# Expert blocks of an attention and mixture-of-experts kernel: the gathered inputs are transposed by VectorE instead of TensorE

## Chip, cores and metric

The kernel runs on one core of one Trainium2 chip. The metric is the device time of one execution in microseconds. Time before: 920.09 us, the median of six runs (919.37 to 922.16).

## What is computed

The reference is one layer in fp32 on `x` of shape (4, 1024, 256): cross attention with a residual, then a mixture of experts with a residual. Only the second half matters here. Of nine experts each token takes the two with the highest probabilities, with weights that add to one:

```python
xf = x.reshape(T, H)                      # layer-normalised, T = 4096, H = 256
cw = zeros((T, E)).at[arange(T)[:, None], idxf].add(wf)      # E = 9, two entries per token
gate = silu(einsum('th,ehi->tei', xf, Wg))                   # i = 704
hidden = gate * einsum('th,ehi->tei', xf, Wu)
out = einsum('tei,eih,te->th', hidden, Wd, cw)
```

## The kernel before

**Attention stage** (the first 387 us of the span). The tokens go by in 32 steps of 128. After each group of 512 tokens, `choices` finds the two experts of each token, `places` (L936) works out where each token stands in the list of its expert, and GpSimd writes token number and weight there by indirect DMA (L950). The normalised tokens go to a DRAM buffer, `y_d`.

**Expert stage** (from 387 us). The lists are cut into blocks, and each block is worked for one expert. A "pair" block (2 in `blocks[j][0]`) has 256 tokens, a "one" block 128; a "flex" block is a one block whose two halves of 64 tokens belong to two experts. There are 41 in the main order: blocks 0 to 5 are pairs ("early", whose lists are known before the last group's), then fifteen times a pair and a one (blocks 6 to 35), then the pairs 36 to 40. One more flex block, `NBLK`, runs only if the counts ask for it.

Each block j goes through these steps:
- `tokens(j)`: GpSimd gathers the token numbers and weights of the block into `ids`. `inputs(j)`: GpSimd gathers the tokens' rows out of `y_d` into `yin` (L1183), one indirect DMA for each 128 tokens, into one of three buffers. `weights(j)`: SyncE loads the expert's weights, `wgu` and `wd`, in six DMAs. All are issued by `fetch()`, which runs at the start of each block: inputs and weights two blocks ahead, tokens four ahead. GpSimd's queue is in order, and also has the scatters of the lists and of the results.
- `turn(j)` (L1202): TensorE transposes `yin`, which has tokens on partitions, by a product with the identity, in squares of 128 (L1211): four for a pair, two for a one. ScalarE copies them from PSUM (tile `px`) to `xT` (L1214), which has features on partitions and two buffers.
- `hidden_pair(j)` (L1218): for f = 0 to 5, four matmuls (two for f = 5) into `pg` (L1225), Silu on ScalarE (L1231), and the product on VectorE (L1232; L1235 for f = 5) into `hid`. `pg` rotates over five PSUM banks. After each f, `pump()` runs up to six steps of `rest`: the routing of the last 512 tokens and then `late_blocks` (L1054), both chains of small VectorE operations. `rest` is empty at the end of block 4.
- `hidden_one(j)` (L1249): three wide products, `psg`, `psu` and `psb`, with 128 tokens as the stationary operand; Silu, and three products on VectorE, of which the last is L1271. `hidden_turn(j)` (L1275) transposes the result on TensorE (L1282) and copies it to `hid`, one half on ScalarE and one on VectorE (L1285).
- `down(j)` (L1289): the second products into `po` (L1299); VectorE multiplies by the token's weight into `co` (L1302). `adding` (L1331): GpSimd adds `co` to the output rows by indirect DMA (L1334).

The order is written out by hand, and each engine follows its own part of it. A step j of the main loop (L1515) is: `fetch()`, hidden products of block j, `turn(j + 1)`, `split(j + 1)` (two small VectorE operations for a flex block, L1319), `down(j - 1)`, `adding` of block j - 1, and for a one block `hidden_turn(j)`. Block 0 is turned inside the last attention step (L1454) and block 1 just behind it (L1503).

Of the kernel before, what the change touches and what calls it, by code (L numbers as in the profile page):

```python
# [15 lines left out]
P = 128  # L16
# [5 lines left out]
def kernel(  # L22
# [18 lines left out]
    nc = tc.nc  # L41
# [82 lines left out]
    def mm_tile(name):  # L124
        return ps_mm.tile([P, TB], F32, tag="mm", name=name)
# [230 lines left out]
    with ExitStack() as kvs:  # L356
# [152 lines left out]
        def place_of(n, t):  # L509

            k, q = divmod(n, N2)
            return (2 * q + t) * 2 + k
# [133 lines left out]
        for n in range(NP):  # L646
# [6 lines left out]
            for c in range(C):  # L653
                for t in range(2):
# [6 lines left out]
                    h = place_of(n, t)  # L661
# [431 lines left out]
    blocks = [(2, i, "early") for i in range(EARLY)]  # L1093
# [12 lines left out]
    hids, wds, yins, ids = [], [], [], []  # L1106
    late = {}

    def of(tiles, j):

        return tiles[j % len(tiles)] if j < NBLK else late[id(tiles)]
# [45 lines left out]
    def weights_upper(j):  # L1157

        _, i, kind = blocks[j]
        if kind == "flex":  # L1160
            load(tabs[kind][0][0:1, 2 * i + 1 : 2 * i + 2], late["w2"], late["d2"])

    def load(number, w, d):
        e = nc.values_load(number, engines=[mybir.EngineType.SP], min_val=0, max_val=E - 1)
        wg_v = wg.rearrange("e (c p) f -> e p c f", p=P)[bass.ds(e, 1)].rearrange("o p c f -> (o p) c f")
        wu_v = wu.rearrange("e (c p) f -> e p c f", p=P)[bass.ds(e, 1)].rearrange("o p c f -> (o p) c f")


        nc.sync.dma_start(out=w[:, :, 0:FF], in_=wg_v)
        nc.sync.dma_start(out=w[:, :, FF : FF + FT], in_=wu_v[:, :, NF * P :])  # L1170
        nc.sync.dma_start(out=w[:, :, FF + FT : FF + FB], in_=wu_v[:, :, FA : NF * P])
        nc.sync.dma_start(out=w[:, :, FF + FB :], in_=wu_v[:, :, 0:FA])
        nc.sync.dma_start(
            out=d[:, 0:NF, :],
            in_=wd[bass.ds(e, 1), 0 : NF * P, :].rearrange("o (f p) d -> p (o f) d", p=P),
        )
        nc.sync.dma_start(
            out=d[64:128, NF, :], in_=wd[bass.ds(e, 1), NF * P : FF, :].rearrange("o p d -> (o p) d")
        )
# [8 lines left out]
    def tokens(j):  # L1188

        nh, i, kind = blocks[j]  # L1190
        got = gather(
            ids[j].rearrange("p h t -> p (h t)"), lists[nh], tabs[kind][1][:, i : i + 1]
        )
        if j in (0, EARLY):
            after(got, sent, "all places of the lists")
# [3 lines left out]
            bound = TOK if j >= EARLY else G_EARLY * TB  # L1199
            gather(of(yins, j)[:, h, :], y_d[:bound, :], ids[j][:, h, 0:1], bound)  # L1200

    def turn(j):  # L1202

        nh = blocks[j][0]
        xT = xTs[j] = late["xT"] if j >= NBLK else pools["spool"].tile(
            [P, C, TS], F32, tag="xT", name=f"xT{j}"
        )
        px = ps_sc.tile([P, TB], F32, tag="sc0", name=f"px{j}").rearrange("p (c t) -> p c t", c=C)
        for c in range(C):
            for h in range(nh):  # L1210
                nc.tensor.transpose(  # L1211
                    px[:, c, h * P : (h + 1) * P], of(yins, j)[:, h, c * P : (c + 1) * P], ident
                )
        nc.scalar.copy(xT[:, :, : nh * P], px[:, :, : nh * P])  # L1214

    UP = [FF + FB + f * P for f in range(FA // P)] + [FF + FT + f * P for f in range(NF - FA // P)]

    def hidden_pair(j, also={}):  # L1218

        (w,), xT, hid = wgus.pop(j), xTs.pop(j), hids[j % 2]  # L1220
        for f in range(NF + 1):
            pg = mm_tile(f"pg{j}_{f}").rearrange("p (g t) -> p g t", g=2)
            for g, at in enumerate((f * P, UP[f]) if f < NF else (f * P,)):
                for c in range(C):
                    nc.tensor.matmul(  # L1225
                        pg[:, g, :], w[:, c, at : at + P], xT[:, c, :],
                        start=(c == 0), stop=(c == C - 1),
                    )
            sl = pools["spool"].tile([P, TS], F32, tag="sl", name=f"sl{j}_{f}")
            if f < NF:  # L1230
                nc.scalar.activation(sl, pg[:, 0, :], AF.Silu)  # L1231
                nc.vector.tensor_tensor(hid[:, f, :], pg[:, 1, :], sl, ALU.mult)  # L1232
            else:
                nc.scalar.activation(sl[64:128, :], pg[0:64, 0, :], AF.Silu)
                nc.vector.tensor_tensor(  # L1235
                    hid[64:128, NF, :], pg[64:128, 0, :], sl[64:128, :], ALU.mult
                )
            pump()
            for fn in also.get(f, ()):
                fn()  # L1240

# [2 lines left out]
    def lanes(of_experts):  # L1244

        n = P // len(of_experts)
        return [slice(h * n, (h + 1) * n) for h in range(len(of_experts))]

    def hidden_one(j):  # L1249


        ws, xT = wgus.pop(j), xTs.pop(j)
        hs = hss[j] = late["hs"] if j >= NBLK else pools["spool"].tile(
            [P, FF], F32, tag="hs", name=f"hs{j}", bufs=1
        )
        pgs = {}
        for k, (at, n) in (("g", (0, FA)), ("u", (FF + FB, FA)), ("b", (FA, 2 * FB))):
            pgs[k] = mm_tile(f"ps{k}{j}")
            for c in range(C):
                for w, rows in zip(ws, lanes(ws)):  # L1260
                    nc.tensor.matmul(
                        pgs[k][rows, :n], xT[:, c, rows], w[:, c, at : at + n],
                        start=(c == 0), stop=(c == C - 1),
                    )
        nc.scalar.activation(hs[:, :FA], pgs["g"], AF.Silu)
        nc.vector.tensor_tensor(hs[:, :FA], pgs["u"], hs[:, :FA], ALU.mult)
        nc.scalar.activation(hs[:, FA:], pgs["b"][:, :FB], AF.Silu)
        nc.vector.tensor_tensor(
            hs[:, FA : NF * P], pgs["b"][:, FB + FT : 2 * FB], hs[:, FA : NF * P], ALU.mult
        )  # L1270
        nc.vector.tensor_tensor(  # L1271
            hs[:, NF * P :], pgs["b"][:, FB : FB + FT], hs[:, NF * P :], ALU.mult
        )
# [53 lines left out]
    def rounds_of(j):  # L1327
        n = 2 if blocks[j][2] == "flex" else 1
        return [(j, rows) for rows in lanes(range(n))]
# [18 lines left out]
    def pump():  # L1348

        if held[0]:  # L1350
            held[0] -= 1
            return
        for _ in range(STEP if rest else 0):
            got = next(rest[0], None)
            if got is None:
                rest.pop(0)
                if not rest:
                    fetch()
                return
            if got is PRODUCT:  # L1360
                held[0] = HOLD
                return
# [3 lines left out]
    def fetch():  # L1366

        end = NBLK if late_ready() else EARLY
        for name, fn, lead in (
            ("weights", weights, LEAD), ("weights_upper", weights_upper, LEAD + 1),  # L1370
            ("inputs", inputs, LEAD), ("tokens", tokens, LEAD + 2),
        ):
            if name == "inputs":

                while ahead["tokens"] < min(now[0] + LEAD + 1, end):
                    tokens(ahead["tokens"])
                    ahead["tokens"] += 1
            while ahead[name] < min(now[0] + lead + 1, end):
                fn(ahead[name])
                ahead[name] += 1  # L1380
# [8 lines left out]
    def advance(what, n=None):  # L1389

        for _ in range(n) if n is not None else iter(int, 1):
            if next(what, None) is None:
                return True
        return False
# [18 lines left out]
    for i in range(N_SUB + 1):  # L1413
        g, s = divmod(i, NS)
        now_on = i < N_SUB
        q = g - 1
# [98 lines left out]
    for j in range(LAST):  # L1515
        now[0] = j
        if j == EARLY:
            assert not rest
            open_late()
        fetch()  # L1520
        if j == EARLY + 1:
            count = nc.values_load(
                tabs["flex_total"][0:1, 0:1], min_val=0, max_val=2 * FLEX
            )
        if j == RARE_AT - 1:
            tokens(NBLK)
            inputs(NBLK)
        if j == RARE_AT:
            weights(NBLK)
            weights_upper(NBLK)  # L1530
        if blocks[j][0] == 2:
            hidden_pair(j)
        else:
            hidden_one(j)
        if j:
            turn(j + 1)
            split(j + 1)
            down(j - 1)
            for r in rounds_of(j - 1):
                adding(*r)  # L1540
        if blocks[j][0] == 1:
            hidden_turn(j)
        if j == RARE_AT:
            split(NBLK)

            with tc.If(count > 2 * (FLEX - RARE)):  # L1546
                turn(NBLK)
                hidden_one(NBLK)
                hidden_turn(NBLK)
                down(NBLK)  # L1550
            for r in rounds_of(NBLK):
                adding(*r)
# [37 lines left out]
```

## Time and profile before

| | |
|---|---|
| median of six runs | 920.09 us (919.37 to 922.16) |
| the profiled execution's own time | 917.93 us |
| its span (first to last instruction) | 916.2 us |
| mean granted TensorE clock | 0.998 |
| ScalarE copies px to xT | x41, 372 to 618 ns each |
| gathers of yin, issue to landing | 2.7 / 5.0 / 7.2 us (least, median, most) |
| expert stage, 500 to 600 us: busy TensorE, VectorE, ScalarE, GpSimd | 100.0, 25.3, 19.9, 45.3 us |
| same stretch, DMA share and rate | 0.82, 236 GB/s |

PE is TensorE's matmuls, PEld its weight loads, DVE VectorE, ACT ScalarE, POOL GpSimd, SP SyncE. L1211 is line 1211 of the kernel before. A line of a timeline has the start in microseconds, the duration, the engine, the line, the operation, output <- inputs, how many instructions were merged into it, and in brackets the idle time in front of it with what ended that. Every fp32 matmul of the hidden and down products has two records. Tile names are given without the block's number. The slices of the page are 40 equal parts of the span, 22.9 us each.

### The profile page before, as it was taken

How to read it: one execution, taken by the hardware profiler on the slowest of the kernel's cores; microseconds unless marked ns; L12 is line 12 of the kernel's file. 1: busy time of each engine (PE TensorE's matmuls, PEld its weight loads, DVE VectorE, ACT ScalarE, POOL GpSimd, SP SyncE). 2: the span in 40 equal slices, each digit the busy share in tenths (PEclk: the TensorE clock that was granted, in tenths of full speed). 3: DMA queues.
4: the chain of work that ended last, by engine and by line, in shares of the span. 5: the costliest groups of instructions: out<-in, count | busy, mean ns of one | idle time of the engine just before them, and what ended most of it. 6: DMA issues, size and time to landing. Idle time of an engine off the chain costs nothing. (4 is left out here: it accounts for less than half of the span.)

```text
span 916.2 us, 13532 instructions
## 1 busy us (share of the span) xinstructions
PE 900.9 (98%) x4290; PEld 694.7 (76%) x4290; DVE 442.8 (48%) x1310; ACT 334.5 (37%) x1055; POOL 316.3 (35%) x328
## 2 busy tenths in 40 slices
PE   8999999999999999999999999999999999999996
PEld 6647777777777777788888777777778778888885
DVE  5775688878788987654622222222222222222221
ACT  4557556564656557441211212211222222221210
POOL 3000002141404343065554435435435435444422
PEclk9999999999999999999999999999999999999999
DMA  7011010521202600466779769779779777779822
GB/s 264 2 23 41 24 47 25 47 46 24 70 24 66 217 24 25 132 188 153 190 217 291 214 207 309 216 210 318 216 209 306 219 200 224 223 219 315 226 29 23
DMA packets 110374, 137.92 MB, mean 151 GB/s; under 512 B 24663, under 2 KB 80287, under 8 KB 110304
## 3 DMA queue, kind: packets, MB, share of 16 engines
q1 hardware_dynamic: 92746, 119.66, 42.8%
q0 software_dynamic: 17344, 17.26, 10.5%
q8 instruction: 35, 0.57, 0.3%
q14 instruction: 35, 0.29, 0.2%
q10 hardware_dynamic: 214, 0.13, 0.0%
HBM read 119.48 MB, written 18.33 MB: 150 GB/s over the span
## 5 line engine op out<-in xcount | busy, mean ns | idle before, releaser
L1225 PE MATMUL pg<-xT,wgu 128*128 128x256 f32 x1144 | 251.8, 380 | 0.4 <-PEq L1546 0.4
L1225 PEld LDWEIGHTS pg<-xT,wgu 128*128 128x128 f32 x1144 | 216.3, 190 | 28.9 <-issue 0.8
L1299 PE MATMUL po<-wd,hid 128*128 128x256 f32 (+1 forms) x804 | 180.5, 380 | 0.0
L1299 PEld LDWEIGHTS po<-wd,hid 128*128 128x128 f32 (+1 forms) x804 | 147.5, 187 | 21.0 <-issue 0.7
L277 ACT ACTIVATE ex<-psc,mx 128x77 f32<-128x77 f32 x512 | 123.6, 360 | 102.4 <-DVE mx L267 101.2
L1334 POOL DMA_INDIRECT out_dram<-co,ids x63 | 100.7, 1598 | 169.6 <-DVE co L1302 147.8
L950 POOL DMA_INDIRECT list_d<-r_entry,r_pli x64 | 68.8, 1075 | 247.6 <-issue 124.1
L336 PE MATMUL po<-u,aT 128*128 128x265 f32 x640 | 151.7, 391 | 0.4
L263 PE MATMUL psc<-g,zT 128*128 128x462 f32 (+1 forms) x384 | 139.2, 511 | 0.0
L336 PEld LDWEIGHTS po<-u,aT 128*128 128x128 f32 x640 | 118.9, 190 | 23.1 <-ACT aT L325 1.4
L1232 DVE TENSOR_TENSOR hid<-pg,sl 128x256 f32<-128x256 f32 x130 | 55.1, 424 | 160.2 <-ACT sl L1231 160.0
L1231 ACT ACTIVATE sl<-pg 128x256 f32<-128x256 f32 x130 | 49.7, 383 | 218.4 <-PE pg L1225 213.4
L263 PEld LDWEIGHTS psc<-g,zT 128*128 128x128 f32 x384 | 72.5, 190 | 58.1 <-issue 50.5
L1302 DVE TENSOR_SCALAR co<-po,ids 128x256 f32<-128x256 f32 x67 | 32.4, 484 | 136.5 <-PE po L1299 134.3
L1183 POOL DMA_INDIRECT yin<-y_d,ids x67 | 70.3, 1049 | 25.1 <-issue 14.7
L267 DVE TENSOR_REDUCE mx<-psc 128x6 f32<-128x462 f32 (+1 forms) x96 | 55.7, 581 | 19.1 <-PE psc L263 16.4
L297 DVE TENSOR_REDUCE sm<-ex 128x16 f32<-128x1232 f32 x32 | 45.9, 1435 | 36.4 <-ACT ex L277 36.4
L325 ACT COPY aT<-pa 128x512 f32<-128x512 f32 (+1 forms) x96 | 49.4, 553 | 26.3 <-PE pa L317 26.3
L317 PEld LDWEIGHTS pa<-ident,an 128*128 128x128 f32 x320 | 36.7, 141 | 8.1 <-PE po L336 1.4
L317 PE MATMUL pa<-ident,an 128*128 128x128 f32 x320 | 40.3, 273 | 1.0 <-DVE an L301 1.0
L301 DVE TENSOR_TENSOR an<-ex,rs 128x1024 f32<-128x1024 f32 x32 | 39.2, 1225 | 1.1
L1287 ACT COPY hid<-ph 128x384 f32<-128x384 f32 x15 | 7.2, 478 | 73.9 <-PE ph L1282 73.9
(311 smaller groups left out, 803.4 us busy)
## 6 DMA issues: line engine op xcount, KB each, us to landing
wgu<-in_L_ffn_Wg_dram SPq DMA_DIRECT2D x41, 704.0 KB
wd<-in_L_ffn_Wd_dram SPq DMA_DIRECT2D x41, 640.0 KB
wgu<-in_L_ffn_Wu_dram SPq DMA_DIRECT2D x41, 512.0 KB
wgu<-in_L_ffn_Wu_dram SPq DMA_DIRECT2D x41, 128.0 KB
x<-in_x_dram SPq DMA_DIRECT2D x8, 512.0 KB
out_dram<-x SPq DMA_DIRECT2D x8, 512.0 KB
y_d<-y SPq DMA_DIRECT2D x8, 512.0 KB
w<-in_L_ffn_Wg_dram SPq DMA_DIRECT2D x5, 704.0 KB
```

What stands on the lines that cost most here:

```text
L263: nc.tensor.matmul(psc[:, :w], zT[:, c, :], g_sb[i // NS // GPB][:, c, h * J : h * J + w], start=(c == 0), stop=(c == C - 1),)
L267: nc.vector.tensor_reduce(nmx[i][:, h : h + n], psc[:, : n * J].rearrange("p (h j) -> p h j", h=n), AX.X, ALU.max, negate=True,)
L277: nc.scalar.activation(exs[i][:, h + q, :], pscs[k][:, q * J : (q + 1) * J], AF.Exp, bias=nmx[i][:, h + q : h + q + 1],)
L317: nc.tensor.transpose(pa[:, q * P : (q + 1) * P], ans[i][:, (k + q) * P : (k + q + 1) * P], ident)
L336: nc.tensor.matmul(po[:, :DE], aT[:, n, :], u_sb[b][:, n, :], start=(n == 0), stop=(n == KC - 1))
L950: i = nc.gpsimd.indirect_dma_start(out=list_d[:, :], out_offset=bass.IndirectOffsetOnAxis(ap=place_i[:, s : s + 1], axis=0), in_=entries[k ...
L1183: return nc.gpsimd.indirect_dma_start(out=dst, out_offset=None, in_=src, in_offset=bass.IndirectOffsetOnAxis(ap=offsets, axis=0), **kw,)
L1225: nc.tensor.matmul(pg[:, g, :], w[:, c, at : at + P], xT[:, c, :], start=(c == 0), stop=(c == C - 1),)
L1231: nc.scalar.activation(sl, pg[:, 0, :], AF.Silu)
L1232: nc.vector.tensor_tensor(hid[:, f, :], pg[:, 1, :], sl, ALU.mult)
L1299: nc.tensor.matmul(po[rows, :D], hid[:, f, at], d[:, f, :], start=(f == 0), stop=(f == NF))
L1334: i = nc.gpsimd.indirect_dma_start(out=out_r, out_offset=bass.IndirectOffsetOnAxis(ap=rows_of(j, h, rows), axis=0), in_=cos[j][:, h, :], i ...
```

## The change

From block 2 on, `turn(j + 1)` in the main loop is replaced by a generator, `turning(j + 1)`. It issues 16 VectorE transposes, one for each square of 32 partitions by 32 partitions: each instruction reads 32 partitions (tokens a to a + 31) of `yin` and writes 32 partitions (features q to q + 31) of `xT`, for both column halves c and, in a pair, both token halves h. That is 128 elements a partition for a pair, 64 for a one, in runs of 32 (`32x2x2x32` and `32x2x32`).

In front of a pair block's hidden products the generator is created, and after each f from 1 on four of its instructions are issued, behind the product and behind `pump()`; so all 16 are issued after f = 4. In a one block all 16 come after the three products of `hidden_one`. VectorE's part of the order in a one block is then: three products (L1271 the last), 16 transposes of block j + 1, `split`, the `co` products of block j - 1, and the copy of `hidden_turn(j)`. TensorE goes from the hidden products of block j straight to `down(j - 1)`.

Blocks 0 and 1 are still turned by TensorE, and so is `NBLK`.

```diff
+    Q = 32
+    def turning(j):
+        nh, xT = blocks[j][0], turned_tile(j)
+        for a in range(0, P, Q):
+            for q in range(0, P, Q):
+                yield nc.vector.transpose(
+                    xT[q : q + Q].rearrange("p c (h t) -> p h c t", t=P)[:, :nh, :, a : a + Q],
+                    of(yins, j)[a : a + Q].rearrange("p h (c d) -> p h c d", d=P)[
+                        :, :nh, :, q : q + Q
+                    ],
+                )
...
-    def hidden_pair(j, also={}):
+    def hidden_pair(j, also={}, upcoming=iter(())):
...
             pump()
+            if f:
+                advance(upcoming, 4)
             for fn in also.get(f, ()):
...
+        upcoming = turning(j + 1) if j else iter(())
         if blocks[j][0] == 2:
-            hidden_pair(j)
+            hidden_pair(j, upcoming=upcoming)
         else:
             hidden_one(j)
+        advance(upcoming)
         if j:
-            turn(j + 1)
             split(j + 1)
             down(j - 1)
```

`turned_tile(j)` takes the buffer of `xT` as the first lines of `turn` did.

More of the change, by code (lines that the diff above doesn't have):

```diff
@@ L1200, in inputs, with turned_tile @@
             gather(of(yins, j)[:, h, :], y_d[:bound, :], ids[j][:, h, 0:1], bound)
-    def turn(j):
-        nh = blocks[j][0]
+    def turned_tile(j):
         xT = xTs[j] = late["xT"] if j >= NBLK else pools["spool"].tile(
@@ L1207, in turn @@
         )
+        return xT
+    Q = 32
[9 more added lines that the diff above has]
+                )
+    def turn(j):
+        nh, xT = blocks[j][0], turned_tile(j)
         px = ps_sc.tile([P, TB], F32, tag="sc0", name=f"px{j}").rearrange("p (c t) -> p c t", c=C)
```

## The prediction

> **What bounds the kernel now.** The page comes first. TensorE is busy for 98% of the span, VectorE for 48%:
>
> ```profile
> PE 900.9 (98%) x4290; PEld 694.7 (76%) x4290; DVE 442.8 (48%) x1310; ACT 334.5 (37%) x1055; POOL 316.3 (35%) x328
> PE   8999999999999999999999999999999999999996
> DVE  5775688878788987654622222222222222222221
> ```
>
> From slice 16 on (the expert blocks, from 387 us) VectorE has 2 tenths of work beside a full TensorE. Time off TensorE is time off the end, as long as VectorE's new work is never what TensorE waits for. Next, the answer for line 1211, the transposes to be removed:
>
> ```profile
> L1211 PE MATMUL px<-ident,yin x134: 272/273/332, 381.7 to 882.6; 128*128 128x128 f32 x134
>   DMA yin<-y_d,ids: 1.5, 3
> ```
>
> There are 134 of them, and they waited 1.5 us in all for their gather. Then the timeline of one "one" block (block 7), where the new work has its shortest deadline:
>
> ```profile
> 494.24 0.60 PE L1211 MATMUL px<-ident,yin 128*128 128x128 f32 x4
> 494.67 5.35 PE L1299 MATMUL po<-wd,hid 128*128 128x256 f32 x24
> 495.01 0.21 DVE L1271 TENSOR_TENSOR hs<-psb,hs 128x64 f32<-128x64 f32 x1
> 497.47 0.48 DVE L1302 TENSOR_SCALAR co<-po,ids 128x256 f32<-128x256 f32 x1 [2.25 <-PE po L1299]
> 499.86 0.82 PE L1282 MATMUL ph<-ident,hs 128*128 128x128 f32 x6
> 500.51 9.66 PE L1225 MATMUL pg<-xT,wgu 128*128 128x256 f32 x44
> ```
>
> Columns are start, duration, engine, line. From VectorE's last product (ends 495.22) to the next block's first matmul (500.51) there are 5.29 us. Last, the timeline around block 2's gather, on GpSimd and TensorE:
>
> ```profile
> 401.09 1.01 POOL L1183 DMA_INDIRECT yin<-y_d,ids  x1 [0.30 <-issue]
> 407.74 0.30 PE L1211 MATMUL px<-ident,yin 128*128 128x128 f32 x1 [0.64 <-DMA yin<-y_d,ids]
> 408.36 0.55 PE L1211 MATMUL px<-ident,yin 128*128 128x128 f32 x3 [0.32 <-DMA yin<-y_d,ids]
> ```
>
> That gather takes 7.2 us to land (408.3), and TensorE is there just too early for it.
>
> **Removed.** 39 blocks (2 to 40) lose their transposes: 24 pairs with four, 15 ones with two. The starts above put four at 0.43 to 0.44 us of TensorE (494.24 to 494.67), so two at 0.22: 24 x 0.44 + 15 x 0.22 = 13.9 us, plus 1.0 us of block 2's waits. 14.9 us is the ceiling of the gain. ScalarE's 39 copies go too; it is 37% busy and TensorE has 5 us of other work behind each, so they count nothing. The weight loads on SyncE that are put down to waiting for L1211 then wait for the last matmul in front, at most 0.44 us earlier: nothing, since TensorE shows no wait for weights.
>
> **Added: 16 instructions a block on VectorE.** Call the time from one start to the next tau, for a pair (32 partitions, 128 elements each). The trace has no such operation. From below: four independent operations of 256 elements took 1.38 us in all with 0.415 us of the last (L877), so 0.32 us each; minus 128 elements at 1.04 ns that is 0.19. From above: 256 elements at 0.424 us (L1232) plus a gap, 0.45. Nearest is an elementwise operation on 128 elements, 0.29 us. Whether neighbours overlap is read from two independent ones that begin on other partitions (0 to 63, then 64 to 127):
>
> ```profile
> 25.09 0.18 DVE L565 TENSOR_TENSOR cfold<-cfold,shift 64x32 f32<-64x32 f32 x1
> 25.29 0.19 DVE L561 TENSOR_TENSOR cfold<-scale,cq 64x32 f32<-64x32 f32 x1
> ```
>
> They do not: the second starts 0.02 us after the first ends (0.03 at other such pairs). Here every instruction writes other partitions than the one before. So 0.29 + 0.03 = 0.32, and I take tau = 0.33, as rearranged patterns are dearer than plain ones here (L1047: 135 elements, 0.41). Ones have 64 elements: 0.21 + 0.03 + 0.01 = 0.25.
>
> [...]
>
> **"One" blocks (15 times).** The 16 transposes queue behind the products of the block: 495.25 + 16 x 0.33 = 500.53, and 0.2 us until a matmul runs (a waiting one started 0.14 us after its release at L317; its weights are no longer loaded ahead). That is 500.73 against 500.51: 0.22 us later than before, where without a wait it would be 0.43 earlier. 15 x 0.22 = +3.3 us. Behind the transposes stand L1302 (twice) and L1285; scatter and next `down` need them later, so that costs nothing.
>
> **Pair blocks in front of a one (15) and of a pair (the last four).** Four transposes follow each product: 0.44 + 1.32 us in a beat of 1.73. Done some 11 us after the block's start; needed at 12 to 15. All hidden: 15 x -0.22 = -3.3 and 4 x -0.44 = -1.8 us. Block 38's gather lands at 865.3; 6.6 us of queue behind it end at 871.9, TensorE comes at 872.4: just hidden.
>
> **The first blocks.** Here VectorE also has the routing, and the new wait for the gather stands in front of it.
> - Block 1: VectorE reaches the transposes at 403.4 and waits until 408.3. Queued behind: three products (1.3), six steps of `places` (1.2), 16 x 0.33 = 5.3: 416.1; TensorE starts block 2 at 416.3, not at 413.93: +2.4. It was free at 412.3. The scatters that need `places` start at 416.61 anyway.
> - Block 2: nothing late, -0.44: block 3 starts at 431.3 (+2.0).
> - Block 3: the gather issued at 432.14 takes 6.2 us (438.3). Behind it 5.3 + 1.3 + 18 steps of `late_blocks` (3.8) = 10.4: 448.7, TensorE 448.9 instead of 444.38: +4.5.
> - Block 4: VectorE comes 2.5 us behind; from 451.4 five products (2.2), 6.6 of steps and 5.3 of transposes end at 465.5, needed at 463.6: block 5 at 465.7 (+6.2).
> - Block 5: -0.44, so +5.8 at block 6.
>
> **Sum.** 5.8 - 3.3 + 3.3 - 1.8 = +4.0 us. The profiled execution took 917.93 us (span 916.2), 2.2 below the median of 920.09: 921.9 for it, 924.1 for the median. The end (scatters behind the last block) moves along. Each 0.01 us of tau is 240 x 0.01 + 0.3 = 2.7 us; the sum is zero at tau = 0.315.
>
> **The clock.** In block 1 TensorE would idle for 4.0 us (412.3 to 416.3). At the end of the span it stopped at 907.94:
>
> ```profile
> 911.00:912.00 1.00, 0.00 (x0) 0.00 (x0) 0.00 (x0) 0.00 (x0) 0.00 (x0) 0.98 0.80 111
> 912.00:913.00 1.00, 0.00 (x0) 0.00 (x0) 0.00 (x0) 0.00 (x0) 0.00 (x0) 0.50 0.04 5
> ```
>
> The seventh figure behind the window is the granted clock: it fell to half 4.0 us after the last matmul. So this is on the edge; I count nothing, and up to 9.5 us (block 2's hidden matmuls at half speed) into the range. [...]
>
> **Rivals.**
> 1. *Faster: the transposes overlap.* If tau is 0.28 or less, no one-block waits (15 x -0.43 = -6.5) and the first blocks lose 4.2 or less: -7.4 us, 912.7. At 0.19, with 1.4 there, -10.2, 909.9. It decides below 0.30. For: L877's 0.32 us for 256 elements. Against: L565 to L561. 27%.
> 2. *Much slower: two cycles per element.* tau 0.45: each one-block 2.2 us late (+32), the first blocks +11.8: +39, 959. Decides from about 0.40. For: L1047's strided row. Against: these rows are runs of 32 contiguous elements. 12%.
> 3. *No effect*: were the transposes hidden already, TensorE would show idle time beside them; it shows 1.0 us. 4%, at 920.1.
>
> My forecast (tau 0.31 to 0.37: -1.3 to +15) has 57%.
>
> **Numbers.** 0.2% (1.84 us) is about what a measurement of this kernel tells from no change. Faster by more needs tau under 0.308: rival 1 and the forecast's lowest edge, 28%. Within: tau 0.308 to 0.322 and rival 3, 12%. Slower: 60%. The range runs from rival 1's lower end (910) to the forecast at 0.37 with a clock drop (945): what is left out is most of rival 2 and little else.
>
> **What would show it.** Right: transposes of 0.29 to 0.33 us end to start; TensorE waiting 0.2 to 0.6 us for them at the first matmul behind each one-block; block 2 starting near 416.3 and block 6 near 480.4 (before 474.62). Wrong: a step under 0.28 and no wait at the one-blocks; block 6 starting before 476; or, on the other side, waits of 2 us per one-block.

## The result, and the profile after

The changed kernel took 920.7 us in the median (916.04 to 923.51, 40 runs) against 919.41 us for the kernel before on the same chips (82 runs): a ratio of 1.0007 [0.9999, 1.0015], or 0.6 us with an interval from -0.1 to +1.4 (the plain medians are 1.3 us apart). No difference can be measured. One execution in all the runs below, of only_3_5, took 1053.04 us at a mean granted clock of 0.848; no ratio counts it. The profiled execution took 921.47 us (span 919.7, mean granted clock 0.991).

The page of the changed kernel, sections 1, 2 and 5 (in section 5: busy time and mean ns of one, then idle time in front with what ended most of it):

```profile
PE 895.0 (97%) x4164; PEld 685.0 (74%) x4164; DVE 609.2 (66%) x1934; ACT 314.8 (34%) x1016; POOL 315.1 (34%) x328
...
PE   8999999999999999999899999999999999999996
...
DVE  5775688878788887657674656656656666666551
...
L1215 DVE STREAM_TRANSPOSE xT<-yin 32x128 f32<-32x128 f32 (+1 forms) x624 | 172.5, 276 | 24.4 <-DMA yin<-y_d,ids 15.2
```

VectorE went from 443 to 609 us, TensorE only from 900.9 to 895.0, although 126 of its matmuls are gone. The second digit 8 in TensorE's row is slice 19, around block 4. What TensorE waited for in the expert stage, from the changed kernel's waits (us in all, times, longest):

```profile
PE pg L1242 <- issue: 9.2, 4, 3.9
PE pg L1242 <- DVEq L1566: 1.1, 1, 1.1
```

"issue" means that the profile shows no releaser; the timelines show it. DVEq is VectorE's sequencer, and L1566 the branch on the extra flex block. First a steady "one" block (block 7) and the start of block 8 in the changed kernel (L1290 is L1271 of before, L1242 the hidden product):

```profile
504.97 0.21 DVE L1290 TENSOR_TENSOR hs<-psb,hs 128x64 f32<-128x64 f32 x1
505.10 5.04 DVE L1215 STREAM_TRANSPOSE xT<-yin 32x128 f32<-32x128 f32 x16
509.38 0.82 PE L1301 MATMUL ph<-ident,hs 128*128 128x128 f32 x6
510.17 0.88 DVE L1321 TENSOR_SCALAR co<-po,ids 128x256 f32<-128x256 f32 x2
510.19 9.77 PE L1242 MATMUL pg<-xT,wgu 128*128 128x256 f32 x44
```

Sixteen transposes in 5.04 us, so 0.315 us from one start to the next; the first began 0.08 us before L1290 ended, and TensorE began 0.05 us after the last. From the end of L1290 (505.18) to the next block are 5.01 us, where before had 5.29: 0.28 us are won, not 0.22 lost. The matmuls took 9.77 us instead of 9.66: in before the first weight load of L1225 starts at 500.40, 0.11 us ahead of its matmul, and here the first of L1242 starts at 510.19, together with its matmul, for it too waits for the transposition.

Then the first blocks. These are the starts of blocks 0, 2, 4 and 5 in the kernel before (each view ends after 12 us and may cut a line short):

```profile
387.49 4.70 PE L1225 MATMUL pg<-xT,wgu 128*128 128x256 f32 x21
413.93 2.32 PE L1225 MATMUL pg<-xT,wgu 128*128 128x256 f32 x10
444.38 7.93 PE L1225 MATMUL pg<-xT,wgu 128*128 128x256 f32 x36
459.50 4.70 PE L1225 MATMUL pg<-xT,wgu 128*128 128x256 f32 x21
```

In the changed kernel, VectorE's timeline and TensorE's:

```profile
408.37 1.25 DVE L1215 STREAM_TRANSPOSE xT<-yin 32x128 f32<-32x128 f32 x4 [5.15 <-DMA yin<-y_d,ids]
...
414.67 1.26 DVE L1215 STREAM_TRANSPOSE xT<-yin 32x128 f32<-32x128 f32 x4
...
441.04 1.25 DVE L1215 STREAM_TRANSPOSE xT<-yin 32x128 f32<-32x128 f32 x4 [2.95 <-DMA yin<-y_d,ids]
```

```profile
387.32 4.92 PE L1242 MATMUL pg<-xT,wgu 128*128 128x256 f32 x22
...
406.77 5.34 PE L1318 MATMUL po<-wd,hid 128*128 128x256 f32 x24
416.03 10.37 PE L1242 MATMUL pg<-xT,wgu 128*128 128x256 f32 x40 [3.92 <-issue]
...
442.00 5.34 PE L1318 MATMUL po<-wd,hid 128*128 128x256 f32 x24
451.02 12.50 PE L1242 MATMUL pg<-xT,wgu 128*128 128x256 f32 x44 [3.68 <-issue]
...
470.05 9.74 PE L1242 MATMUL pg<-xT,wgu 128*128 128x256 f32 x44 [1.35 <-issue]
```

VectorE waits for both late gathers, and TensorE then waits 3.9, 3.7 and 1.35 us in front of blocks 2, 4 and 5. Blocks 2 and 4 are also slow themselves. Busy time in stretches of the changed kernel, on TensorE (window, its length, matmul time, granted clock, DMA share, GB/s):

```profile
414.00:416.00 2.00, 0.00 (x0) 0.91 0.97 309
...
417.00:419.00 2.00, 2.00 (x6) 0.50 0.02 4
419.00:420.00 1.00, 1.00 (x6) 0.96 0.00 0
448.00:450.00 2.00, 0.00 (x0) 0.95 1.05 383
...
456.00:460.00 4.00, 4.00 (x19) 0.92 0.50 59
```

A mean of 0.91 over 2 us is half clock for the last 0.36 us. So the clock fell at 415.7, 3.6 us after TensorE had run dry (412.1), and was whole again at 419.1, 3.1 us after it had work. In front of block 4 it fell at 449.8, 2.5 us after the last product (447.3), and stayed at half until 456.6, 5.6 us into the work.

Times up to block 0 differ by 4 us between profiled executions (387.1 to 391.5) with no edit in that part. So starts of blocks are compared against before from block 0's start on. A start is that of the block's first hidden matmul in the timeline:

| later than before by, us | block 2 | 3 | 4 | 5 | 6 | 36 | 40 (last) |
|---|---|---|---|---|---|---|---|
| predicted | +2.4 | +2.0 | +4.5 | +6.2 | +5.8 | +5.8 | +4.0 |
| the changed kernel | +2.27 | +3.40 | +6.81 | +10.72 | +10.35 | +4.23 | +3.75 |

From block 6 to 36 it gains 6.12 us: -0.28 or -0.35 at each step from a one block to a pair, and -0.12 to -0.15 at nearly every step from a pair to a one (block 25 alone loses 0.27, where VectorE waited 2.35 us for its gather). Kernels that leave block 2 as it was differ from before by 0.2 to 1.3 us there, always to the early side, most of it because before waited 1.0 us for that gather in its profiled execution; the first blocks' numbers are good to about 1 us, the later steps to a few hundredths.

### The profile page after: what moved, and what is told of

Same layout as the page of the kernel before. It is cut to its first block, busy times and chain, and to the rows that moved or that the text cites. A ratio compares the mean times of both kernels' runs of the same rounds, so it can differ in the third digit from the quotient of the medians.

```text
span 919.7 us, 13855 instructions
## 1 busy us (share of the span) xinstructions
PE 895.0 (97%) x4164; PEld 685.0 (74%) x4164; DVE 609.2 (66%) x1934; ACT 314.8 (34%) x1016; POOL 315.1 (34%) x328
## 5 line engine op out<-in xcount | busy, mean ns | idle before, releaser
L1242 PE MATMUL pg<-xT,wgu 128*128 128x256 f32 x1144 | 257.7, 386 | 10.3 <-issue 9.2
L1242 PEld LDWEIGHTS pg<-xT,wgu 128*128 128x128 f32 x1144 | 219.0, 193 | 44.2 <-issue 12.1
L1215 DVE STREAM_TRANSPOSE xT<-yin 32x128 f32<-32x128 f32 (+1 forms) x624 | 172.5, 276 | 24.4 <-DMA yin<-y_d,ids 15.2
L1318 PEld LDWEIGHTS po<-wd,hid 128*128 128x128 f32 (+1 forms) x804 | 149.9, 187 | 28.0 <-issue 3.7
L317 PEld LDWEIGHTS pa<-ident,an 128*128 128x128 f32 x320 | 36.7, 141 | 8.1 <-PE po L336 1.4
L317 PE MATMUL pa<-ident,an 128*128 128x128 f32 x320 | 40.3, 273 | 1.0 <-DVE an L301 1.0
L1285 DVE TENSOR_TENSOR hs<-psu,hs 128x512 f32<-128x512 f32 x15 | 10.4, 692 | 46.3 <-PE psu L1280 43.4
```

What stands on the lines that cost most here:

```text
L317: nc.tensor.transpose(pa[:, q * P : (q + 1) * P], ans[i][:, (k + q) * P : (k + q + 1) * P], ident)
L1215: yield nc.vector.transpose(xT[q : q + Q].rearrange("p c (h t) -> p h c t", t=P)[:, :nh, :, a : a + Q], of(yins, j)[a : a + Q].rearrange(" ...
L1242: nc.tensor.matmul(pg[:, g, :], w[:, c, at : at + P], xT[:, c, :], start=(c == 0), stop=(c == C - 1),)
L1318: nc.tensor.matmul(po[rows, :D], hid[:, f, at], d[:, f, :], start=(f == 0), stop=(f == NF))
```

## The experiments

All kernels are the changed one with a short edit. Ratios are to the kernel before, run beside them; "from block 0" is read as in the table above.

### The steady blocks

**from6: TensorE transposes blocks 2 to 5 again.** Theory: the steady blocks win, the first ones give it back. Rival: the steady steps are a wash, as predicted.

```diff
-        upcoming = turning(j + 1) if j else iter(())
+        by_vector = j and j + 1 >= EARLY
+        upcoming = turning(j + 1) if by_vector else iter(())
...
         if j:
+            if not by_vector:
+                turn(j + 1)
```

> Blocks 2 to 5 are turned by TensorE again, VectorE takes over from block 6 on. Theory A (the change gains in the steady blocks and gives it back in blocks 2 to 5, where VectorE's queue stands behind a gather): block 6 starts within 0.3 us of its time before, then each pair-to-one step is 0.13 us shorter, each one-to-pair step 0.28, the last pairs 0.5 together: 6.6 us less than before, about 912.8 us. Rival C (there is no gain to be had in the steady blocks, the transposes cost TensorE nothing): 919.4 us, as before, within 1.

Measured: 913.06 us (6 runs), 0.9923 [0.9905, 0.9942]; from block 0 -0.44 at block 6 and -7.27 at the last block. The steps are those of the changed kernel (-0.28 and -0.12 again and again). The steady blocks are worth 6 to 7 us, and the first ones take them back. (The rival is excluded, and with it the prediction's third: TensorE's transposes were not free.)

**behind_ones: only the fifteen pairs behind a one block.** This is the step that the prediction priced at +0.22.

```diff
+        by_vector = j and blocks[j][0] == 1
```

> VectorE turns only the 15 pairs that come behind a one block; TensorE turns the rest. Theory A: each one-to-pair step is 0.28 us shorter than before and the pair blocks that begin with the wait lose 0.10 of it, 15 x 0.18 = 2.7 us: block 6 as before, ratio 0.997, about 917 us. By the prediction's price for this part (0.22 us later per step): 3.3 us above before, 923.

Measured: 916.26 us (12 runs), 0.9969 [0.9955, 0.9983]. Each step from a one block to a pair is -0.27 to -0.35, each following step +0.07 to +0.10: the weights that are no longer loaded ahead. So the pair's transposition is worth -0.18 net, and the next block's, fully hidden, -0.22: together the -0.40 of the changed kernel. A price of +0.22 is excluded, for the kernel would have been slower than before.

**same_part: each transposition writes the partitions that it reads.** The squares land in wrong places, so its expert outputs are not the reference's; the instructions are as many and as large. It is from6 with one slice exchanged, so that runs of four stay on the same 32 partitions.

```diff
-                    xT[q : q + Q].rearrange(...)[:, :nh, :, a : a + Q],
+                    xT[a : a + Q].rearrange(...)[:, :nh, :, q : q + Q],
```

> As from6, but each transpose writes the 32 partitions it reads, in four runs of four, so neighbours begin on the same partitions; the squares land on other places of xT, so the expert outputs are not the reference's. Theory F (a transpose that writes other partitions than the one in front waits for its end): the step falls from 0.31 us to about 0.19 to 0.2 for 128 elements (4 in 0.9 us instead of 1.25), 16 take about 3.3 us instead of 5.0, no one block waits, and the time is 2 to 4 us below from6. Rival G (transposes never overlap): 0.31 us a step and the time of from6.

Measured: 908.35 us (6 runs), 0.9889 [0.9867, 0.991]. The timeline of VectorE in this kernel:

```profile
496.23 3.56 DVE L1215 STREAM_TRANSPOSE xT<-yin 32x128 f32<-32x128 f32 x16
...
505.58 0.60 DVE L1215 STREAM_TRANSPOSE xT<-yin 32x64 f32<-32x64 f32 x4
```

Sixteen take 3.56 us instead of 5.04, four of 64 elements 0.60 instead of 0.97. The same instructions do overlap when their partitions stay the same: what keeps the real ones at 0.315 us is the change of partitions. With 3.56 us no one block waits, and the steps are the full -0.44 (at four places -0.39) and -0.22; only block 39 still loses to its late gather. The single transposes of this kernel show it too: in the sixteen above the three steps that change partitions are 0.27 us long, each beginning 0.01 us after the end of the one in front (0.26 us long), and the other twelve are 0.19 to 0.24. In the changed kernel, where the partitions change with each, every one of a run began 0.01 us after the end of the one in front. The change of partitions costs some 0.1 us here, by 0.315 against 0.196, the median step in this kernel.

**from6_ahead: from6, and in a one block eight of the sixteen go ahead of its products.** They then run while TensorE makes the wide products, where VectorE had nothing to do.

```diff
     def hidden_one(j, upcoming=iter(())):
...
+        advance(upcoming, 8)
         nc.scalar.activation(hs[:, :FA], pgs["g"], AF.Silu)
```

> As from6, and in one blocks 8 of the 16 transposes are issued ahead of the three products instead of behind them, into 3 us in which VectorE waits for TensorE. Theory A with the deadline of the one blocks (each step is 0.15 us short of the 0.43 that TensorE's transposes took): the steps become 0.43 shorter than before, 15 x 0.15 = 2.2 us below from6, about 910.6 us. If the deadline is not what holds them, the same as from6; if the products get late, above it.

Measured: 907.61 us (4 runs), 0.9868 [0.9851, 0.9885]. Block 7 in its timeline:

```profile
490.57 2.51 DVE L1215 STREAM_TRANSPOSE xT<-yin 32x128 f32<-32x128 f32 x8 [0.27 <-DVE co L1322]
...
495.11 0.21 DVE L1291 TENSOR_TENSOR hs<-psb,hs 128x64 f32<-128x64 f32 x1
495.35 2.52 DVE L1215 STREAM_TRANSPOSE xT<-yin 32x128 f32<-32x128 f32 x8
...
500.17 5.99 PE L1242 MATMUL pg<-xT,wgu 128*128 128x256 f32 x27
```

The last transposition ends at 497.87, 2.3 us before TensorE comes, and the steady steps are the whole -0.44 (at four places -0.39) or -0.22. Two steps lose: block 25 +0.34 and block 39 +1.47, because VectorE arrives 2.65 and 5.52 us ahead of those blocks' gathers. From block 0 it is at -9.69 at the last block, 2.4 below from6, as expected. The medians lie 5.4 apart, more than that: all four executions here had a mean granted clock of 0.998, but only two of from6's six (910.6 us), while the other four were at 0.996 (914.05).

**best: from6_ahead, and block 39 on TensorE too.**

```diff
-        by_vector = j and j + 1 >= EARLY
+        by_vector = j and j + 1 >= EARLY and j + 1 != LAST - 1
```

> As from6_ahead, and block 39 is turned by TensorE too: in from6_ahead its gather lands at 858.1 us of the span, VectorE waits 5.5 us for it and TensorE 1.7 us for VectorE. With TensorE turning it behind the hidden products, the wait is 0.5 us and the step 0.44: about 1 us below from6_ahead, 906 to 907 us, the lowest of all. If the late gather is not what holds block 39: the same as from6_ahead.

Measured: 907.34 us (907.04 to 907.63, 4 runs), 0.9872 [0.9847, 0.9897], and from block 0 no step above zero from block 6 on (-12.63 at the last block, 1.27 of it in front of block 2). It cannot be told from from6_ahead by the medians; both beat before by 1.3%, or 12 us. Against before's executions at a clock of 0.997 or more alone (median 918.1, see below) it is 11 us, and its steps from block 2 to the last give 11.4.

### The first blocks

**first4: only blocks 2 to 5 on VectorE**, the complement of from6.

```diff
-        by_vector = j and j + 1 >= EARLY
+        by_vector = j and j + 1 < EARLY
```

> The other part alone: VectorE turns blocks 2 to 5, TensorE all from block 6 on. Theory A: block 6 starts some 10 us late (6 where the granted clock holds) and nothing is given back: about 927 us, 6.6 above the changed kernel. Rival C: 920 to 921, as the changed kernel. Rival D (the loss at block 6 is caught up later by the transfers, whatever turns the blocks): under 923.

Measured: 926.18 us (6 runs), 1.0083 [1.0065, 1.0102]; from block 0 +6.49 at block 6, and +7.17 at the end. With from6 it adds up to nothing: -0.1 by these starts, and +6.6 with -6.5 by the medians. (The changed kernel's own profiled execution, at +3.75, has a second fall of the clock.) Its four waits on TensorE are 2.65, 1.65, 0.94 and 1.33 us, and the clock fell once, at 416.1 us, when block 2 had been running for 0.8.

**keep_clock: the changed kernel with 14 products of the identity behind `down(0)` and `down(2)`**, so that TensorE is busy while it waits.

```diff
             down(j - 1)
+            if j in (1, 3):
+                keep = ps_sc.tile([P, TB], F32, tag="sc0", name=f"keep{j}")
+                for _ in range(14):
+                    nc.tensor.matmul(keep[:, :P], ident, ident, start=True, stop=True)
```

> The changed kernel, with 14 matmuls of 128x128 on the identity (3.0 us, results unused) on TensorE behind the down products of blocks 0 and 2, inside the two idle times of 3.9 and 3.7 us. Theory B (a part of the loss is the granted clock, which fell to half in both idle times): hidden products of block 2 take 9.7 us instead of 11.3, those of block 4 9.7 instead of 12.5; block 6 starts about 4.3 us earlier than in the profiled execution of the changed kernel; the median falls by 2 to 4 us, to 917 to 919, and the spread over executions (916.0 to 923.5) narrows. Rival (the idle times alone are the loss): same starts, 920.7 us within 1.

Measured: 919.83 us (12 runs), 1.0004 [0.9994, 1.0014]. The clock stayed whole in the expert stage, and the hidden products of blocks 2 and 4 took 9.9 and 9.7 us from first to last, as in before; from block 0 +6.66 at block 6 instead of +10.35. But the median is only 0.9 below the changed kernel's, where 2 to 4 were expected. Its TensorE now waits where it did not before, in front of block 3 (434.76):

```profile
434.76 9.73 PE L1242 MATMUL pg<-xT,wgu 128*128 128x256 f32 x44 [1.79 <-issue]
468.82 9.74 PE L1242 MATMUL pg<-xT,wgu 128*128 128x256 f32 x44 [1.34 <-issue]
```

In the changed kernel the slow block 2 gave VectorE the time for block 3's transposes; with a whole clock TensorE waits for them instead (block 3 at +3.20 against +3.40). In these two profiles it is the fall in front of block 4 that costs time. Why the median gives back only 0.9 of these 3.7 us is taken up below.

**late: in blocks 1 to 4 all sixteen go behind the block's last product and its steps.** If the loss came only from what is queued behind the wait for the gather, this would end it.

```diff
-            if f:
+            if f and j >= EARLY - 1:
                 advance(upcoming, 4)
```

> The changed kernel, but in blocks 1 to 4 all 16 transposes are issued behind the last product and the last steps of the block, so that nothing of the block stands behind the wait for the gather. Theory A (the loss in the first blocks is what is queued behind the wait, products and steps, beside the 16 transposes themselves): counted from block 0's start, block 2 starts within 0.6 us of its time before (gather at 408.3, 16 x 0.31 = 5.0, against TensorE at 412.3), block 4 some 2 us late, block 6 at +1 to +3 instead of +6.7 to +10.4, with no or one fall of the clock: 914 to 918 us. Rival E (the wait for the gather and the 5.0 us of transposes are the loss, whatever the order): block 6 at +6 or more, about 920.

Measured: 924.23 us (12 runs), 1.0055 [1.0039, 1.0071], so slower than the changed kernel. The loss at block 2 is gone (-0.17; TensorE still waits 1.48 us there, about what before's waits and transposes took), and block 3 is 3.94 us late instead. The clock also fell in the wait in front of block 3, whose products took 12.06 us, 2.4 more than in before. VectorE's timeline of late, and TensorE's:

```profile
432.01 0.18 DVE L996 TENSOR_SCALAR pair_ef<-pair_ef 128x20 f32<-128x20 f32 x1
432.10 5.04 DVE L1215 STREAM_TRANSPOSE xT<-yin 32x128 f32<-32x128 f32 x16
```

```profile
437.24 12.06 PE L1242 MATMUL pg<-xT,wgu 128*128 128x256 f32 x44 [4.31 <-issue]
```

No gather holds these transposes; products and routing steps run up to 432.1. The expectation failed: the queue behind the wait is not the only cause.

**only_3_5 and only_2_4: VectorE has two of the four blocks.** The gathers of 3 and 5 land in time, those of 2 and 4 late.

```diff
+        by_vector = j and j + 1 in (3, 5)      # only_3_5
+        by_vector = j and j + 1 in (2, 4)      # only_2_4
```

> VectorE transposes only the inputs of blocks 3 and 5; all other blocks are TensorE's. The gathers of these two blocks land in time in the kernel before (TensorE's transposes of them waited for nothing). Theory W (the first blocks cost only because the wait for the gathers of blocks 2 and 4 stands in front of VectorE's work): block 3 begins 0.44 us earlier against before, counted from block 0's start, block 5 0.88 earlier, the median is 918.5 to 919.2. Theory L (VectorE's own load in block 4, products, routing steps and 16 transposes, is longer than TensorE's block): block 3 0.44 earlier; in block 4 VectorE has 2.2 us of products, 6.6 of steps and 5.0 of transposes, 13.8 us from the first product about 1.2 us after the block's start, against 14.9 us of TensorE until block 5: -0.4 to +1.5 at block 5, median 919 to 921. Prediction's own working (block 3's load free, -0.44; block 4's hidden work ends in time when VectorE doesn't come in late): -0.88.

Measured: 918.74 us (10 runs), 1.0 [0.9987, 1.0012]; from block 0 -0.60 at block 3, +1.07 at block 5. The median fits the first theory as well; the starts decide. VectorE's timeline of only_3_5 in front of block 5, and TensorE's:

```profile
458.61 0.15 DVE L1081 CAST flex_total<-flex_sum 128x1 int32<-128x1 f32 x1
458.78 1.26 DVE L1215 STREAM_TRANSPOSE xT<-yin 32x128 f32<-32x128 f32 x4
```

```profile
460.14 2.18 PE L1242 MATMUL pg<-xT,wgu 128*128 128x256 f32 x9 [1.46 <-issue]
```

From 447.92 to 460.04 VectorE has no gap: products, steps and transposes. Its load alone makes block 5 late, by 1.17 us in this step. (Block 4 is 0.50 late because TensorE, 0.4 us early, met that block's late gather itself.)

> VectorE transposes only the inputs of blocks 2 and 4, whose gathers land late; all others are TensorE's. Theory W (wait for the gathers): the whole loss of the first blocks is here: block 2 at +2.1, block 4 at +4.5 against before, and block 6 at +4.5 to +6.5 (to +10 with the clock down in both idle times), counted from block 0's start; median 924 to 927. Theory L (the load of VectorE in whichever block): about half of it, +2 to +3 at block 6, median 922. The two kernels' shifts add up to the first blocks' shift of the kernel that gives VectorE blocks 2 to 5 (+6.5) only if nothing is carried from one block to the next.

Measured: 928.33 us (4 runs), 1.0092 [1.007, 1.0114]; from block 0 +1.54 at block 2, +6.44 at block 4, +8.08 at block 6. The wait behind block 1 in VectorE's timeline of only_2_4, and what TensorE makes of it:

```profile
405.24 0.76 DVE L1249 TENSOR_TENSOR hid<-pg,sl 128x256 f32<-128x256 f32 x2
410.43 1.25 DVE L1215 STREAM_TRANSPOSE xT<-yin 32x128 f32<-32x128 f32 x4 [4.44 <-DMA yin<-y_d,ids]
```

```profile
418.08 10.56 PE L1242 MATMUL pg<-xT,wgu 128*128 128x256 f32 x40 [3.19 <-issue]
453.43 11.31 PE L1242 MATMUL pg<-xT,wgu 128*128 128x256 f32 x44 [3.41 <-issue]
```

The clock fell at 419.1, 1.0 us after the first wait, and at 453.2, in the second; blocks 2 and 4 ran 1.8 and 1.7 us longer for it (3.4 of the 8.08). Without them 4.7 us are left, against 1.2 for blocks 3 and 5: the blocks behind the late gathers carry most of the first blocks' loss, and VectorE's load makes a smaller part that needs no late gather.

## Why the prediction was wrong

The outline was the right one: a gain in the steady blocks, a loss in the first blocks where VectorE waits for gathers ahead of other work, and a sum near nothing. But the one blocks' term had the wrong sign. "Slower" at 60% rested on a sum of +4.0; +0.6 (0.0007 of 919.41) was measured. Term by term:

1. **"500.73 against 500.51: 0.22 us later", fifteen times.** This is the step that failed, by 0.50 us each or 7.5 in all: -0.28 was measured at most of them. Three readings made it: tau was 0.315 and not 0.33 (0.24 us over sixteen); the start behind the last one was 0.05 us and not 0.2, which had been borrowed from L317; and the first transposition starts 0.08 us ahead of L1290's end, where 0.03 behind it was assumed (0.11). behind_ones shows it by itself.
2. **Pairs in front of a one, -0.22 each.** Measured -0.12 to -0.15, 1.6 us less in all with the 0.27 that block 25 lost, for the pair block in which they are made began without its weights loaded ahead and ran 0.1 us longer. The prediction named the lost preload, but only as a part of its 0.2 us.
3. **The first blocks, +5.8.** With a whole clock keep_clock has +6.66 and first4, with one fall, +6.49: about the right size, within the 1 us these starts are good for. But the prediction had block 3's work as "nothing late"; its +2.0 was +3.2 in keep_clock, where TensorE waits 1.79 us. VectorE's steps were priced behind the wait, not as a load that fills the whole block.
4. **"I count nothing" for the clock.** The prediction took the one row of before, a fall 4.0 us after the last matmul, as the edge, and looked at block 1's idle time alone; the clock fell there and in front of block 4. In the profiled execution it cost 3.7 us at block 6 (+10.35 against keep_clock's +6.66). Blocks 2 and 4 ran 1.6 and 2.8 us longer, which is half of the 3.1 and 5.6 us of work at half clock; the first of these took the place of a wait. The 9.5 us in the range was the price of a whole block at half speed.

The last four pairs gave -0.5 and not -1.8: 0.33 lost at block 37, where VectorE's queue stands at the branch on the flex block (the wait on DVEq, 1.1 us), and the gain of block 39 lost to the gather that was called "just hidden". That gather landed at 870.2, 4.9 us later than the 865.3 of before, where the blocks around it were 3.95 later.

The prediction's own formula gives zero at tau = 0.315, which is what was measured, and the time did not change. That is partly luck: the formula reaches zero with nothing won in the steady blocks but the pairs' 5.1 us, whereas the chip won 6.6 there and lost more in front. And the profiled execution's +3.5 (921.47 against 917.93) agrees with the forecast of 921.9 only because a missing gain and a missing loss cancelled: by its starts it is +10.35, then -6.12, then -0.48, in all +3.75, where +5.8, 0 and -1.8 had been added up to +4.0.

**The rivals.** Rival 1, overlap with tau of 0.28 or less, is false as it was stated, and same_part shows why: L877, its evidence (0.32 us a step), works on the same partitions each time; L565 and L561, on changing ones (the second 0.02 us after the end of the first), were the right rows. But the consequence that it drew, no loss at the one blocks, came half true by another way. Rival 2 (a tau of 0.45) is excluded by 0.315. Rival 3 (no effect) has the right time by a wrong cause: from6, at 0.9923, excludes transposes that cost nothing.

**What stays open.** By the two profiled executions the changed kernel is 3.5 us behind; by the ratio 0.6. 2.3 us of the 3.5 are the choice of executions: before's lies 1.5 under its median, the changed kernel's 0.8 above its own. The mean granted clock of its executions was 0.990 to 0.995: those at 0.994 took 916.0 to 917.8 us, those at 0.991 or less 919.4 to 923.5. keep_clock's were 0.995 to 0.998, as were before's beside it. So the clock is lower in the changed kernel's executions, by an amount that varies; but from6's profile shows a granted clock of 0.66 from 10 to 15 us, in the loads at the start, and its block 0 begins 3.7 us later than before's, with no help of the expert blocks. Six of the twelve profiles have such a fall, before and the changed kernel not: those begin block 0 at 389.4 to 391.5 us, the others at 387.1 to 389.5. Before's executions split in the same way. Of 52 whose clock is on record, 26 were at 0.997 or more (median 918.1 us) and 26 at 0.996 or less (920.0). Nor does the clock order the kernels: keep_clock's five executions at 0.998 have a median of 919.6, above the changed kernel's six at 0.994 (916.2). So the 3.7 us of the fourth point are what two profiled executions show, and why a whole clock is worth only 0.9 us in the median stays open.

## What to carry to other kernels

Moving work from the engine that bounds to an idle one is worth what the idle engine can finish before its next deadline, block by block: here 11 to 12 us were to be had in 34 blocks, and four blocks with a busy VectorE, two of them with a late gather, took all that the plain move won. Before a wait is moved to an engine that works in the order written (VectorE waited 5.15 us for block 2's gather here, with three products and six routing steps behind it), list what stands behind it, and move only those blocks whose data are there and for which the engine has time; then split the moved work so that half of it goes into the gap ahead of the block's own products.

## What was not expected of the hardware

- VectorE's transposes of 32 partitions and 128 elements (0.303 us each in the median) followed at 0.315 us in the changed kernel, where the partitions change with each, and at 0.196 in the median in same_part, where they change with every fourth; with 64 elements four took 0.97 and 0.60 us.
- The clock's fall came 2.5, 3.6 and 4.0 us after the last product (the last at the end of before), and in first4 and only_2_4 0.8 and 1.0 us after TensorE had begun again, so how long TensorE has been idle does not set it alone. The two stretches at half clock were 3.413 and 6.827 us long (415.66 to 419.07, 449.79 to 456.62), one being twice the other. The changes in the changed kernel's profile also lie on one grid: 415.66, 419.07, 449.79, 456.62 and 914.00 us are 1, 9, 2 and 134 times 3.413 us apart. In the 3.413 us in front of its three falls (the third at the end) TensorE had been busy for a share of 0.00, 0.28 and 0.27; in the other stretches of this grid at full clock, from 388 us on, for 0.60 or more. In front of the fall in first4 it was 0.22, of the two in only_2_4 0.30 and 0.06. So 2.65 us of idle time were enough in first4, and 2.59 us in front of block 4 of late were not (its products took 9.73 us, as at a whole clock).
- Where the moving operand (`xT`) came late, the product also lost the early load of its stationary one, though those weights are fetched two blocks ahead: in front of block 8 of the changed kernel the first load began with the product, at 510.19, where before has it 0.11 us ahead, and the block took 9.77 us instead of 9.66.
